# Seven sequences and one, a four-batch first run, and a half-size inverse transform in a long-convolution layer with routed experts

## The chip, the cores and the metric

The kernel runs on one core of a Trainium2 chip. Its engines are TensorE (PE in the profile; its weight loads are PEld), VectorE (DVE), ScalarE (ACT), GpSimd (POOL) and SyncE (SP, which here only starts transfers). Each engine works through its own list of instructions in order, and they meet through semaphores. The metric is the device time of one execution in microseconds. The kernel before has a median of 708.53 us over six executions, from 697.98 to 713.18.

## The reference, cut to what matters

Eight sequences of 512 tokens and 256 channels go through a gated long convolution and then a mixture of 16 experts of which each token uses 4, each with a residual and a layer norm:

```python
def layer(x):                                    # 8 x 512 x 256, float32
    u = short_conv(x @ W_in + b_in)              # 768 channels, three taps
    x0, x1, v = split(u, 3)
    k = sin-MLP filter, 512 x 256                # the same for every sequence
    y = (irfft(rfft(v * x1) * conj(rfft(k)), 1024)[:512] + filter_bias) * x0
    x = layernorm(x + y @ W_out + b_out)
    w, e = top_4(softmax(x @ gate.T))            # weights made to sum to 1
    out = sum_k w_k * (silu(x @ w1[e_k].T) * (x @ w3[e_k].T)) @ w2[e_k].T
    out += (silu(x @ sw1.T) * (x @ sw3.T)) @ sw2.T    # the shared expert
    return layernorm(x + out)
```

## The kernel before, in words

**The first half, per sequence.** `front` (from L436) projects the transposed input to 768 channels in blocks of 128 (`u_ps`, L413), applies the three taps on ScalarE and VectorE (L396 to L402), multiplies to get v, turns it (`vt_ps`, L456) and takes a forward transform as matmuls with a table of cosines and sines (`v_ps`, L479). `product` (L498 to L529) multiplies by the filter's spectrum on VectorE; its result `pf` has two halves, c = 0 and c = 1, that belong to the two halves of the 512 positions. `convolved_full` (L537) is the inverse transform: for each of two blocks of 128 channels and each half c, four float32 matmuls with a moving operand of 256 columns from the table `inv4_sb` (L547). `gated_y`, `normed` and `scaled` multiply by x0, project with W_out (`z_ps`, L630) and normalise to x1.

**Routing.** `turned` and `heads` turn x1 and compute the gate and the shared expert (`x1t_ps` L663, `hs_ps` L678, `os_ps` L782). `router` takes the top four, `route` counts how many rows each expert has got (`r_ps`, L821), and `scatter` sends each token's row to four places in HBM with 16 indirect transfers of GpSimd (L960), into a region `xs` per set in which every expert has its own stretch of rows.

**Sets and batches.** `SPLIT` (L27) groups sequences into sets, and the sequences of a set into batches. A set has its own `xs` and its own table of results in HBM. When a batch but the last of a set is routed, only tiles of 128 rows that are already full are computed; the last batch takes what remains, with partly filled tiles. `slots()` counts them: 17, 32 and 62 tiles for the batches of the first set (sequences 0 to 5), and 47 for the second set (6 and 7), 158 in all.

**The experts.** `fetch` (L1096) loads four tiles at a time (`xr`), waiting for one of two buffers. `expert_pair` handles two tiles, a pair: four transposes (`xr_ps`, L1150), eight matmul passes with w1 and w3 (`h_ps`, L1164), silu on ScalarE into `act` (L1175), a product on VectorE (L1178), two transposes of `act` back into `h_ps` (L1184), a copy to `actt` (L1189), four passes with w2 (`o_ps`, L1196), a scaling with the routing weight into `o` (L1207 or L1209), and per tile one indirect transfer to the results (L1218). `act` and `actt` have three buffers each.

**The return.** When all pairs of a set have written their results, `returned` loads for each of its sequences four blocks `got` of 512 KB (L1258), adds the four contributions of each token to the shared expert's sum, normalises and stores (`out_x`, L1307). The sum of a sequence in the first set is meanwhile kept in HBM (`kept`, L798; read back at L1242); the last set's stays on the chip. In the last set odd blocks are added by TensorE (`s_ps`, L1269).

**What sets the order.** The order on every engine is worked out when the program is built: each step names its engine, an estimated cost, what it needs and which buffers it takes, and a planner (`Plan.run`) repeatedly picks the step that can start first, and among near equals the one of lowest rank. A sequence b has rank 2 + b/100; the pairs of a batch have the rank in `late`, so that the first batch's pairs stand behind the front of sequence 3 and ahead of that of sequence 4, the second's ahead of sequence 6, the last two behind sequence 7. Nine buffers of 4 KB per partition, `b4`, serve many uses (inputs, v, y, sums, `got` and others).

Of the kernel before, what the change touches and what calls it, by code (L numbers as in the profile page):

```python
# [13 lines left out]
F32 = mybir.dt.float32  # L14
# [6 lines left out]
P = 128  # L21
# [5 lines left out]
SPLIT = (((0, 1), (2, 3), (4, 5)), ((6, 7),))  # L27
OUTRANK = 0.5
KD = D // P
# [173 lines left out]
def layer(  # L203
# [20 lines left out]
    fwd: bass.AP,  # L224
    inv4: bass.AP,
# [35 lines left out]
    plan.ring(h=4, xr=2, sel=6, xrt=3, act=3, actt=3, ob=4, at=4)  # L261
# [54 lines left out]
    load(inv4_sb, inv4.rearrange("(k p) t -> p k t", p=P), "inv4")  # L316
    b_out_sb = const.tile([P, D], F32, name="b_out_sb")
# [180 lines left out]
    def product(b, vf, hf_):  # L498
# [15 lines left out]
        plan.done(("pf", b, 0))  # L514
        plan.spawn(convolved_full(b, pf, hp), 2 + b * 0.01)
# [12 lines left out]
        plan.let(hf_)  # L528
        plan.done(("pf", b, 1))  # L529

# [6 lines left out]
    def convolved_full(b, pf, hp):  # L537
        for i in range(KD):
            for c in range(2):
                rings = [*(["ps"] if c == 0 else []), *(["b4:y"] if i == c == 0 else [])]  # L540
                yield turn("PE", 8 * PASS[CH], [("pf", b, c), "inv4"], rings)
                if i == c == 0:
                    y, hy = sb("b4:y", 0, [P, KD, T], f"y_{b}")
                if c == 0:
                    y_ps, h = ps([P, T], f"y_ps_{b}_{i}")
                for k in range(4):
                    nc.tensor.matmul(  # L547
                        y_ps[:, c * CH : (c + 1) * CH],
                        lhsT=pf[:, k // 2, k % 2, c, i * P : (i + 1) * P],
                        rhs=inv4_sb[:, k, :],  # L550
                        start=k == 0,
                        stop=k == 3,
                    )
# [519 lines left out]
    late = [2 + b * 0.01 - 0.005 for b in (4, 6, 8, 9)]  # L1073
# [51 lines left out]
    def expert_pair(p, f, xr4, hxr):  # L1125
# [48 lines left out]
        act, hact = sb("act", 3, [P, 2, HE], f"act_{p}", home=home)  # L1174
# [12 lines left out]
        actt, hat = sb("actt", 3, [P, 2, P], f"actt_{p}", home=home)  # L1187
# [141 lines left out]
def shape_constants():  # L1329
# [28 lines left out]
    found = {"places": places, "tri": tri, "seg": np.concatenate(seg), "pos": pos, "decay": decay, "fwd": fwd, "inv4": inv4, "sign": np.stack([even, -even], 1)}  # L1358
# [40 lines left out]
```

## Time and profile before

| | |
|---|---|
| median of six executions | 708.53 us (697.98 to 713.18) |
| the profiled execution | 709.05 us, with a span of 707.3 us |
| mean granted TensorE clock | 0.921 |
| PE busy | 587.0 us (83% of the span) |
| DVE / ACT / POOL busy | 458.2 / 366.8 / 319.9 us |
| moved by DMA | 114.08 MB, 161 GB/s over the span |
| last routing matmul (`r_ps`, sequence 7) | at 476.7 us |
| first load of `got` | at 589.88 us |
| last expert matmul | ends at 673.85 us |

The profile is one execution on the chip. Times are microseconds from the start of the span unless marked ns. A busy PE is not a PE at its peak: its matmuls are pipelined, and the granted clock can halve, so the distance from the start of one group of matmuls to the start of the next is a better price than the mean duration of one. A float32 matmul runs as two passes, and the profile counts passes; a transpose is one pass. The 1.75 us between the span and the execution's own time lie around the span.

### The profile page before, as it was taken

Reading aid. Unit: us, or ns where it says so; the run is one execution under the profiler, and the core shown is the slowest. Engines: PE = TensorE matmul, PEld = TensorE weight load, DVE = VectorE, ACT = ScalarE, POOL = GpSimd, SP = SyncE. Lnnn points to the kernel's source line nnn. Section 1 sums busy time; section 2 is a strip of 40 time slices with the busy share of each in tenths; the row PEclk is TensorE's granted clock in tenths of the full one; section 3 lists DMA queues with packets and bytes.
Section 4 is the critical chain, followed back from the end, with each engine's and each line's share of the span. In section 5 each row is a group of like instructions: output and inputs, shape, how many; then the busy total and the mean of one; then the engine's idle time right before and its main releaser. Section 6 shows DMA issues by size and latency. Waiting matters only on the chain.

```text
span 707.3 us, 10010 instructions
## 1 busy us (share of the span) xinstructions
PE 587.0 (83%) x2508; PEld 448.1 (63%) x2508; DVE 458.2 (65%) x1271; ACT 366.8 (52%) x810; POOL 319.9 (45%) x588
## 2 busy tenths in 40 slices
PE   6979798987969699979598996796787999899724
PEld 2437484845748577767466785685676877787612
DVE  4998989998759459958472586346132234777754
ACT  3416465654455276754242760472242445898855
POOL 0000007373563474376676238347556655456540
PEclk9999999996989799989799999798899999899968
DMA  8991003234341153335563424225524456979855
GB/s 274 355 341 36 30 31 143 81 114 148 116 152 56 62 177 125 105 149 195 174 210 119 152 88 161 75 85 203 186 96 144 139 147 207 302 264 310 310 186 205
DMA packets 67686, 114.08 MB, mean 161 GB/s; under 512 B 11547, under 2 KB 48425, under 8 KB 67630
## 3 DMA queue, kind: packets, MB, share of 16 engines
q1 hardware_dynamic: 53902, 77.75, 34.6%
q0 software_dynamic: 13728, 35.69, 13.4%
q8 instruction: 22, 0.36, 0.2%
q14 instruction: 34, 0.28, 0.1%
HBM read 61.25 MB, written 56.07 MB: 166 GB/s over the span
## 4 chain that ended last, share of the span: by engine, by line
PE 56%; DVE 15%; another core or an unknown queue 7%; ACT 7%; issue 6%; DMA 5%; POOL 3%; SPq 1%; ACTq 0%; POOLq 0%; DVEq 0%
PE h_ps L1164 13%; PE o_ps L1196 9%; PE y_ps L547 7%; PE u_ps L413 6%; PE hs_ps L678 4%; PE z_ps L630 4%; DMA got<-results 4%; PE xr_ps L1150 3%; PE v_ps L479 3%; PE h_ps L1184 2%; POOL results L1218 1%; POOL xs L960 1%; ACT unused L589 1%; PE os_ps L782 1%
## 5 line engine op out<-in xcount | busy, mean ns | idle before, releaser
L1218 POOL DMA_INDIRECT results<-o,to x158 | 161.6, 1023 | 161.5 <-ACT o L1207 63.4
L960 POOL DMA_INDIRECT xs<-x,at x128 | 135.3, 1057 | 198.6 <-DVE cx L402 106.3
L1164 PE MATMUL h_ps<-w_sb,xrt 128*128 x632 | 154.6, 391 | 12.4 <-ACT xrt L1155 10.6
L1164 PEld LDWEIGHTS h_ps<-w_sb,xrt 128*128 128x128 f32 x632 | 120.4, 197 | 31.5 <-ACT xrt L1155 12.5
L1196 PE MATMUL o_ps<-w_sb,actt 128*128 x316 | 91.0, 424 | 41.3 <-ACT actt L1189 29.5
L1196 PEld LDWEIGHTS o_ps<-w_sb,actt 128*128 128x128 f32 x316 | 63.1, 210 | 56.2 <-ACT actt L1189 34.5
L413 PE MATMUL u_ps<-xt,w_in_sb 128*128 128x512 f32 x192 | 88.8, 604 | 4.1 <-DMA xt<-in_x_t 4.1
L1178 DVE TENSOR_TENSOR act<-act,h_ps 128x256 f32<-128x256 f32 (+1 forms) x80 | 31.9, 414 | 92.7 <-ACT act L1175 67.7
L1175 ACT ACTIVATE act<-h_ps 128x256 f32<-128x256 f32 (+1 forms) x80 | 29.9, 382 | 96.8 <-remote 40.7
L547 PE MATMUL y_ps<-inv_sb,pf 128*128 128x256 f32 x256 | 65.2, 411 | 11.7 <-DVE pf L526 9.7
L396 ACT ACTIVATE u<-u_ps,chan_sb 128x512 f32<-128x512 f32 x48 | 33.1, 689 | 72.6 <-DVE v L402 32.5
L547 PEld LDWEIGHTS y_ps<-inv_sb,pf 128*128 128x128 f32 x256 | 52.4, 208 | 23.8 <-DVE pf L526 11.0
L1155 ACT COPY xrt<-xr_ps 128x512 f32<-128x512 f32 (+1 forms) x80 | 45.3, 586 | 41.4 <-PE xr_ps L1150 14.7
L413 PEld LDWEIGHTS u_ps<-xt,w_in_sb 128*128 128x128 f32 x192 | 35.9, 193 | 42.7 <-issue 41.2
L1150 PE MATMUL xr_ps<-ident,xr 128*128 128x128 f32 x316 | 47.4, 283 | 1.7 <-ACT xrt L1155 0.7
L1207 ACT ACTIVATE o<-o_ps,sel 128x256 f32<-128x256 f32 x84 | 35.0, 470 | 26.5 <-PE o_ps L1196 18.8
L1209 DVE TENSOR_TENSOR o<-o_ps,sel 128x512 f32<-128x512 f32 x37 | 25.5, 690 | 34.4 <-PE o_ps L1196 17.9
L678 PE MATMUL hs_ps<-w_sb,x1t 128*128 128x272 f32 x128 | 37.2, 449 | 10.1 <-ACT x1t L431 5.8
L1150 PEld LDWEIGHTS xr_ps<-ident,xr 128*128 128x128 f32 x316 | 39.4, 147 | 9.6 <-issue 4.1
L1189 ACT COPY actt<-h_ps 128x256 f32<-128x256 f32 (+1 forms) x80 | 28.3, 378 | 29.8 <-remote 15.0
L1184 PE MATMUL h_ps<-ident,act 128*128 128x128 f32 x158 | 30.6, 292 | 12.5 <-issue 8.2
L678 PEld LDWEIGHTS hs_ps<-w_sb,x1t 128*128 128x128 f32 x128 | 27.5, 219 | 18.0 <-ACT x1t L431 6.5
(179 smaller groups left out, 943.9 us busy)
## 6 DMA issues: line engine op xcount, KB each, us to landing
xr<-xs SPq DMA_DIRECT2D x158, 144.0 KB
got<-results SPq DMA_DIRECT2D x32, 512.0 KB
xs<-blank SPq DMA_DIRECT2D x62, 144.0 KB
w_sb<-in_experts SPq DMA_DIRECT2D x17, 384.0 KB
xt<-in_x_t SPq DMA_DIRECT2D x8, 512.0 KB
xn<-in_x SPq DMA_DIRECT2D x8, 512.0 KB
kept<-acc SPq DMA_DIRECT2D x6, 512.0 KB
sum<-kept SPq DMA_DIRECT2D x6, 512.0 KB
```

The lines of the kernel that those rows point to most:

```text
L396: nc.scalar.activation(u, u_ps, AF.Identity, bias=chan_sb[:, m, 3:4])
L413: nc.tensor.matmul(u_ps, lhsT=w_in_sb[:, k, m * P : (m + 1) * P], rhs=xt[:, k, :], start=k == 0, stop=k == KD - 1)
L547: nc.tensor.matmul(y_ps[:, c * CH : (c + 1) * CH], lhsT=pf[:, k // 2, k % 2, c, i * P : (i + 1) * P], rhs=inv4_sb[:, k, :], start=k == 0, ...
L678: nc.tensor.matmul(h_ps, lhsT=x1t[:, k, q * P : (q + 1) * P], rhs=w_sb[:, k, NE * D :], start=k == 0, stop=k == KD - 1,)
L960: move = nc.gpsimd.indirect_dma_start(out=xs[i], out_offset=bass.IndirectOffsetOnAxis(ap=at[:, q, k : k + 1], axis=0), in_=x1[:, q, :], in ...
L1150: nc.tensor.transpose(t_ps[:, j, k, :], xr[:, j, k * P : (k + 1) * P], ident)
L1155: nc.scalar.copy(xrt[:, :n], t_ps[:, :n])
L1164: nc.tensor.matmul(h_ps[:, j, :], lhsT=xrt[:, j, k, :], rhs=w_sb[:, k, bass.ds(at[j], D)], start=k == 0, stop=k == KD - 1,)
L1184: nc.tensor.transpose(a_ps[:, j, :], act[:, j, :], ident)
L1196: nc.tensor.matmul(o_ps[:, j, :], lhsT=actt[:, j, :], rhs=w_sb[:, 2, bass.ds(at[j], D)], start=True, stop=True)
L1207: nc.scalar.activation(o[:, j], o_ps[:, j], AF.Copy, scale=sel[:, j0 + j, 0:1])
L1218: move = nc.gpsimd.indirect_dma_start(out=results[i], out_offset=bass.IndirectOffsetOnAxis(ap=to[:, j0 + j : j0 + j + 1], axis=0), in_=o[: ...
```

## The change

Three edits. The sets become seven sequences and one, with the first set in four batches; from sequence 3 on (`FULL = 3`) the inverse transform uses the sum and the difference of the two halves of `pf`, with half as many columns per matmul; and `act` and `actt` have two buffers instead of three, which is the room that the second table takes. The tiles per batch are now 17, 32, 32 and 46 for the first set and 31 for the second, again 158. `late` gets one more rank: the third batch's pairs stand ahead of the front of sequence 7.

```diff
-SPLIT = (((0, 1), (2, 3), (4, 5)), ((6, 7),))
+SPLIT = (((0, 1), (2, 3), (4, 5), (6,)), ((7,),))
+FULL = 3
...
-    plan.ring(h=4, xr=2, sel=6, xrt=3, act=3, actt=3, ob=4, at=4)
+    plan.ring(h=4, xr=2, sel=6, xrt=3, act=2, actt=2, ob=4, at=4)
...
     load(inv4_sb, inv4.rearrange("(k p) t -> p k t", p=P), "inv4")
+    inv_sb = const.tile([P, 2, CH], F32, name="inv_sb")
+    load(inv_sb, inv.rearrange("(k p) t -> p k t", p=P), "inv")
...
-        plan.done(("pf", b, 0))
-        plan.spawn(convolved_full(b, pf, hp), 2 + b * 0.01)
+        if b < FULL:
+            plan.done(("pf", b, 0))
+            plan.spawn(convolved_full(b, pf, hp), 2 + b * 0.01)
...
+        if b < FULL:
+            plan.done(("pf", b, 1))
+            return
+
+        yield turn("DVE", 2 * 1.22, (), ["b4:pe"])
+        pe, he = sb("b4:pe", 0, [P, 2, 2, D], f"pe_{b}")
+        nc.vector.tensor_tensor(pe, pf[:, :, 0], pf[:, :, 1], ALU.add)
+        plan.done(("pf", b, 0))
+        nc.vector.tensor_tensor(pf[:, :, 0], pf[:, :, 0], pf[:, :, 1], ALU.subtract)
         plan.done(("pf", b, 1))
+        plan.spawn(convolved(b, (pe, pf[:, :, 0]), (he, hp)), 2 + b * 0.01)
...
+    def convolved(b, sums, held):
+        for i in range(KD):
+            for k in range(2):
+                rings = [*(["ps"] if k == 0 else []), *(["b4:y"] if i == k == 0 else [])]
+                yield turn("PE", 8 * PASS[P], [("pf", b, k), "inv"], rings)
+                if i == k == 0:
+                    y, hy = sb("b4:y", 0, [P, KD, T], f"y_{b}")
+                if k == 0:
+                    y_ps, h = ps([P, T], f"y_ps_{b}_{i}")
+                for c in range(2):
+                    for part in range(2):
+                        nc.tensor.matmul(
+                            y_ps[:, c * CH + k : (c + 1) * CH : 2],
+                            lhsT=sums[k][:, part, c, i * P : (i + 1) * P],
+                            rhs=inv_sb[:, part, k * P : (k + 1) * P],
+                            start=part == 0,
+                            stop=part == 1,
+                        )
+            plan.done(("y_ps", b, i))
+            plan.spawn(gated_y(b, i, y, y_ps, h), 2 + b * 0.01)
+        plan.let(*held)
+        plan.spawn(normed(b, y, hy), 2 + b * 0.01)
...
-    late = [2 + b * 0.01 - 0.005 for b in (4, 6, 8, 9)]
+    late = [2 + b * 0.01 - 0.005 for b in (4, 6, 7, 8, 9)]
...
-        act, hact = sb("act", 3, [P, 2, HE], f"act_{p}", home=home)
+        act, hact = sb("act", 2, [P, 2, HE], f"act_{p}", home=home)
...
-        actt, hat = sb("actt", 3, [P, 2, P], f"actt_{p}", home=home)
+        actt, hat = sb("actt", 2, [P, 2, P], f"actt_{p}", home=home)
```

The order that comes out of the planner differs between the two programs from sequence 3 on. In the order of TensorE, the pairs whose `h_ps` matmuls stand ahead of the routing matmuls of sequence 7 are 35 before and 41 after. In the order of SP, the first set's last fetch is followed by four fetches of the second set, and then the loads of `got` begin, in both programs. Before, 8 fetches and 24 loads of `got` for the first set follow, 16 of these loads ahead of the last fetch and 8 behind it; then 8 loads for the second set. After, 4 fetches and 28 loads follow, 11 ahead of the last fetch and 17 behind it; then 4 loads for the second set.

More of the change, by code (lines that the diff above doesn't have):

```diff
@@ L224, in layer @@
     fwd: bass.AP,
+    inv: bass.AP,
     inv4: bass.AP,
@@ L1357, in shape_constants @@
     places = np.concatenate([TOPK * (QT * p + np.arange(QT)) - spare, spare], 1)
[L1358 removed]
+    found = {"places": places, "tri": tri, "seg": np.concatenate(seg), "pos": pos, "decay": decay, "fwd": fwd, "inv": fwd.T / CH, "inv4": inv4, "sign": np.stack([even, -even], 1)}
     return {k: np.ascontiguousarray(v, f32) for k, v in found.items()}
```

## The prediction

> **What bounds the kernel now.** I read the page's busy times and slices first, then the busy time by stage, then single stretches of the timeline.
>
> ```profile
> PE 587.0 (83%) x2508; PEld 448.1 (63%) x2508; DVE 458.2 (65%) x1271; ACT 366.8 (52%) x810; POOL 319.9 (45%) x588
> ...
> PE   6979798987969699979598996796787999899724
> ...
> DMA  8991003234341153335563424225524456979855
> ```
>
> TensorE is the busiest, but no single engine holds for the whole span, so I cut it where the work changes: end of the front-only stretch, routing of sequence 7 (476.4), first load of results (589.9), last fetch (650.7), last expert matmul (673.9).
>
> ```profile
> core 0: us, PE busy (x) PEld busy (x) DVE busy (x) ACT busy (x) POOL busy (x), PEclk, DMA share, GB/s
> 0.00:175.00 175.00, 151.10 (x488) 94.77 (x489) 153.49 (x351) 87.76 (x168) 38.91 (x76) 0.93 0.47 156
> 175.00:476.40 301.40, 259.55 (x1171) 207.02 (x1170) 189.90 (x558) 150.81 (x340) 160.76 (x291) 0.92 0.38 129
> 476.40:589.90 113.50, 92.61 (x450) 77.66 (x449) 37.86 (x112) 41.06 (x98) 69.04 (x131) 0.92 0.47 149
> 589.90:650.70 60.80, 55.00 (x277) 46.21 (x276) 45.04 (x141) 49.88 (x109) 31.80 (x57) 0.94 0.87 291
> 673.90:707.30 33.40, 9.87 (x32) 7.19 (x32) 16.01 (x62) 16.90 (x48) 5.78 (x9) 0.76 0.53 190
> ```
>
> See three regimes. Until 175 VectorE and TensorE are both near full (153.5 and 151.1 of 175). From 175 to 590 TensorE leads (259.6 of 301.4, then 92.6 of 113.5). From 590 on DMA moves 291 GB/s at a share of 0.87 beside the experts, and from 673.9 the rest is the return of results alone. The chain of waits agrees: in its last part its two longest pieces are loads of `got`, 3.69 us at 681.81 and 9.56 us at 687.16.
>
> **The halved inverse transform.** Prices come from distances of starts at full clock:
>
> ```profile
> 273.87 5.34 PE L547 MATMUL y_ps<-inv_sb,pf 128*128 128x256 f32 x24
> 279.05 3.83 PE L678 MATMUL hs_ps<-w_sb,x1t 128*128 128x272 f32 x16
> ...
> 286.45 0.60 PE L1150 MATMUL xr_ps<-ident,xr 128*128 128x128 f32 x4
> 286.89 1.88 PE L413 MATMUL u_ps<-xt,w_in_sb 128*128 128x512 f32 x4
> ```
>
> 24 passes of 256 columns take 279.05 - 273.87 = 5.18 us, 0.216 each; 4 passes of 128 columns take 0.44, 0.11 each. A sequence has 32 passes before and after, so 6.9 us becomes 3.5. For the sequences 3 to 7 that is 5 x 3.45 = 17.2 us less on TensorE, all of it ahead of the routing of sequence 7. No trace row shows a float32 product of 128 columns written to every second column: below, the 0.098 of the routing passes of 64 columns (4 in 0.39 us at 104.57) would give 18.9; above, an unchanged 0.216 gives 0. I take 0.11, the nearest row in width, with fresh weights in each pass as here.
>
> A rule speaks against it. The Trainium skill, "TensorE: Matmul & The Clock Gate", section "Back-to-back issue gap", says that in a stream of weight loads and matmuls the spacing does not shrink in proportion to the columns: 81 ns per matmul at 128 where the isolated formula has 56 (109 at 256). By that shape this edit would save about 28 parts in 109, an estimate of 9 us instead of 17.2, and the forecast would rise by 8. The rows above, 0.11 against 0.216 with a load in each pass, do not show such a floor.
>
> VectorE gets two additions of 128x1024 per sequence, 1.22 us each by the filter products at L507 (eight, mean 1224 ns): 2.44 us. For sequence 3 they fall into the stretch where VectorE is full: +2.4 on the path. For the other four VectorE is busy 190 of 301 us and they hide; with that cover gone they cost 4 x 2.44 = 9.8. The matmuls also wait for the whole product instead of its first half, 9 operations of 0.69 us plus 1.22, 7.4 us later; expert pairs stand between in TensorE's order, so I take 0; without pairs it is at most 7.4 for each of five, 37.
>
> The second table adds 256 KB at the start. At 301 GB/s (the first 25 us) that is 0.9 us on every load behind it; the only wait for a load in the list of waits of the first 64 us ends at 8.05, for a load that SP issues earlier, so 0, at most 0.9.
>
> **Two buffers for act.** Read a steady pair of pairs:
>
> ```profile
> 560.72 1.89 PE L1164 MATMUL h_ps<-w_sb,xrt 128*128 x8
> 562.45 0.38 PE L1184 MATMUL h_ps<-ident,act 128*128 128x128 f32 x2
> 562.66 1.04 PE L1150 MATMUL xr_ps<-ident,xr 128*128 128x128 f32 x8
> 563.54 1.03 PE L1196 MATMUL o_ps<-w_sb,actt 128*128 x4
> 564.40 0.38 PE L1184 MATMUL h_ps<-ident,act 128*128 128x128 f32 x2
> ```
>
> A pair is 1.73 (`h_ps`) + 0.21 (back transposes) + 0.44 (half of the 0.88) + 0.86 (`o_ps`) = 3.24 us of TensorE. A buffer is held from silu (0.38) over the product (0.41) to the back transposes; two buffers allow two periods, 6.5 us, and that covers it: 0. If the cover is gone a silu that waits also holds what stands behind it on ScalarE, copies of `xrt` and `actt` and evictions, for which TensorE waits; up to 0.38 on each of 80 pairs is 30 us. Below nothing there is no reason for a gain.
>
> **Sets of seven and one.** Tiles stay 158 and pairs 80, so the experts cost the same. What moves is the border: the first set's pairs grow from 56 to 64 and the second's shrink from 24 to 16. Loads of results begin when the first set is through, 8 pairs later in TensorE's order: 8 x 3.24 = 25.9. So the first load moves from 589.9 to 589.9 + 25.9 - 17.2 + 2.4 = 601.0.
>
> From there SP's order decides. In it the loads stand among fetches, which wait for TensorE (waits of SP for `xr_ps` make 107.2 us in total):
>
> ```profile
> 589.88 0.83 SPq L1258 DMA_DIRECT2D got<-results  x2
> ...
> 648.69 1.37 SPq L1096 DMA_DIRECT2D xr<-xs  x3
> ...
> 663.56 6.03 SPq L1258 DMA_DIRECT2D got<-results  x4
> 673.41 4.49 SPq L1307 DMA_DIRECT2D out_x<-sum  x2
> 681.81 2.33 SPq L1258 DMA_DIRECT2D got<-results  x5
> ```
>
> Before, eight fetches take 58.8 us (589.9 to 648.7), 7.35 each; after there are four: 29.4, to 630.4, with 11 loads done. Behind the last fetch, before, 8 loads of the first set go out from 650.7 to 669.6, 2.4 us each, with one reload of a sum among them; after, 17 loads: 40.8, and a reload more than in proportion, 512 KB at 297 GB/s, 1.8: 673.0. The second set's pairs are done by then: 13.5 pairs remain at the first load (21.5 before, in 83 us, 3.86 each), so 601 + 52 = 653 and their writes some 8 us later (673.85 to 681.8 before). So the wait for them at 681.81 goes, and the return of the first set is what is late next. Then 4 loads instead of 8: from 681.81 to 696.73 eight took 14.9, 1.9 each, so 7.5, and 3.7 from issue to use (681.81 to 685.52): 684.2. From the last block's use to the end it is 10.6 (696.75 to 707.3), as before. Span 694.8; with 1.75 around it, **697 us**, against 709.05 of this execution, 1.7% less. The execution stands 0.5 us above the median, so I leave it.
>
> **Rivals.**
> - *The first set's return becomes the tail and is slow.* Before, six sequences took from 589.9 to 681.8, 15.3 us each. My sum has (673.0 - 601.0) / 7 = 10.3. At 15.3 the span ends at 601.0 + 107.1 + 7.5 + 3.7 + 10.6 = 729.9: **732**. It decides from 12.0 us per sequence on, where the end equals 709; over 14.1 it is slower by 2%. For it: ScalarE is busy 49.9 of 60.8 us in that stretch, and stores wait in SP's order ahead of loads. Against it: behind the last fetch 8 loads took 18.9, and half of ScalarE's work there is the experts', which end early.
> - *TensorE's time is not the bound, or the change does not halve it.* If strided writes keep 0.216, or stalls eat the gain, 17.2 returns: **714**.
> - *Stalls shrink.* Between 175 and 476 the chain has three pieces put down to an unknown queue, 9.99 us at 192.56, 7.78 at 232.08 and 13.70 at 432.18, beside runs of indirect transfers on GpSimd. A new order may meet two of them with TensorE full, some 17 us: **680**. It may as well make two more: 714, the case above. The runs of `scatter` are still eight.
>
> **How the numbers follow.** Forecast 0.46, stalls shrink 0.22, gain lost 0.17, slow return 0.15. The forecast's own spread is about 8 us either way. From 678 to 720 leaves out the slow return and the edges of the others, about 0.2; the unhidden bounds (9.8, 30, 37) lie in the cases above 709. The six times before spread over 15 us, so 2%, 694.4 to 722.7, is about what can be told from no change. Faster by more: most of 680 and some two fifths of the forecast, 0.39. Slower by more: most of 732 and a little of 714, 0.13. Within: 0.48.
>
> **What will show it.** `y_ps` passes of the later sequences at 0.11 us; last `r_ps` near 481 (6 more pairs ahead of it, 19.4, less 17.2, plus 2.4); first load of `got` near 601; last expert matmul near 653, then some 40 us with TensorE idle; no wait for `results` ahead of the last four loads. It is wrong if the first load comes much after 605, if loads behind the last fetch take over 3 us each, or if `act` waits for back transposes appear on ScalarE.

## The result and the profile after

The changed kernel takes 717.64 us in the median of 36 executions (703.84 to 726.03); 78 executions of the kernel before have a median of 707.46 us (697.44 to 715.47). The ratio is 1.0101, with a 95% interval of 1.0070 to 1.0132. It goes by the executions within 1.5% of each kernel's fastest; the medians of all, and the spans of the two profiled executions, lie some 10 us apart. The forecast was 697, a ratio of 0.984: the change was to win 11.5 us and, by the ratio, loses some 7.

The page of the changed kernel: busy time of each engine, then the slices of TensorE and of DMA, then the shares of the chain that ended last.

```profile
PE 570.9 (80%) x2492; PEld 435.6 (61%) x2492; DVE 470.5 (66%) x1302; ACT 365.4 (51%) x815; POOL 320.4 (45%) x588
...
PE   5979798994969598299788998688677998977503
...
DMA  8991004234252244414332535563553543599785
...
PE 50%; DVE 17%; another core or an unknown queue 10%; ACT 9%; issue 7%; DMA 3%; POOL 2%; SPq 1%; ACTq 0%; DVEq 0%; POOLq 0%
```

TensorE has lost 16.1 us of work (587.0 to 570.9) and VectorE has gained 12.3, as the edits say. But the span has grown from 707.3 to 717.7, so TensorE's idle time grew by 26 us. TensorE's row of slices, which before has no digit below 5 until the last two, now has a 4 in the tenth and a 2 in the seventeenth (287 to 305 us), and the share of the chain put down to an unknown queue went from 7% to 10%.

Busy time of each engine by stage, cut at the same events as in the prediction (routing of sequence 7, first load of `got`, and 684, behind which TensorE has almost nothing left):

```profile
core 0: us, PE busy (x) PEld busy (x) DVE busy (x) ACT busy (x) POOL busy (x), PEclk, DMA share, GB/s
0.00:175.00 175.00, 145.38 (x473) 89.86 (x474) 153.95 (x343) 84.89 (x164) 38.83 (x76) 0.94 0.49 157
175.00:499.60 324.60, 270.26 (x1293) 217.31 (x1293) 206.55 (x601) 165.54 (x375) 176.47 (x319) 0.91 0.41 134
499.60:621.70 122.10, 104.35 (x505) 88.21 (x505) 40.09 (x127) 46.23 (x114) 73.08 (x139) 0.90 0.46 144
621.70:684.00 62.30, 45.50 (x209) 35.98 (x207) 46.23 (x148) 49.30 (x111) 29.71 (x53) 0.90 0.85 286
684.00:717.70 33.70, 5.45 (x16) 4.20 (x16) 23.64 (x86) 19.46 (x54) 2.27 (x3) 0.60 0.75 269
```

The stage from 175 to the last routing is where the loss sits: 324.6 us where the forecast had 306 (to 481), with 54.3 us in which TensorE is idle, against 41.8 before. From there on the stages are near the forecast: 122.1 to the first load (forecast 120), 96.0 from the first load to the end (forecast 93.8).

The halved transform did what it says. The timeline of TensorE shows eight passes in each line:

```profile
176.28 1.05 PE L585 MATMUL y_ps<-inv_sb,pe 128*128 128x128 f32 x8
177.17 1.06 PE L585 MATMUL y_ps<-inv_sb,pf 128*128 128x128 f32 x8
178.06 1.06 PE L585 MATMUL y_ps<-inv_sb,pe 128*128 128x128 f32 x8
```

0.89 us from start to start for eight passes, 0.11 each. And this is the largest of the new stalls, from the timeline of all engines (start, length, engine and line, and in brackets the idle time ahead and what released it):

```profile
290.90 0.60 PE L1188 MATMUL xr_ps<-ident,xr 128*128 128x128 f32 x4
...
292.79 0.44 PE L1222 MATMUL h_ps<-ident,act 128*128 128x128 f32 x2 [1.29 <-issue]
...
301.47 0.96 POOL L998 DMA_INDIRECT xs<-x,at  x1 [0.22 <-issue]
...
304.64 0.59 ACT L1193 COPY xrt<-xr_ps 128x512 f32<-128x512 f32 x1 [14.29 <-remote]
...
305.28 2.07 PE L585 MATMUL y_ps<-inv_sb,pe 128*128 128x128 f32 x8 [12.05 <-ACT xrt L1193]
```

The four transposes end at 291.5. ScalarE's copy of them starts at 304.64, 2.2 us after the end of a run of 15 indirect transfers of GpSimd (283.1 to 302.4); "remote" means that the profile sees no instruction that ended just then. TensorE, next in line, waits 12.05 us for the copy. The trace of before has such waits too (the prediction's third rival names three). Waits of ScalarE and VectorE of more than 1 us with this label make 85 us before and 98 us after.

### The profile page after: what moved, and what is told of

The parts are those of the page before. It is cut to its first block, busy times and chain, and to the rows that moved or that the text cites. A ratio compares the mean times of both kernels' runs of the same rounds, so it can differ in the third digit from the quotient of the medians.

```text
span 717.7 us, 10077 instructions
## 1 busy us (share of the span) xinstructions
PE 570.9 (80%) x2492; PEld 435.6 (61%) x2492; DVE 470.5 (66%) x1302; ACT 365.4 (51%) x815; POOL 320.4 (45%) x588
## 4 chain that ended last, share of the span: by engine, by line
PE 50%; DVE 17%; another core or an unknown queue 10%; ACT 9%; issue 7%; DMA 3%; POOL 2%; SPq 1%; ACTq 0%; DVEq 0%; POOLq 0%
PE h_ps L1202 12%; PE o_ps L1234 9%; PE u_ps L417 6%; PE z_ps L668 4%; PE hs_ps L716 3%; PE xr_ps L1188 3%; PE y_ps L562 3%; PE y_ps L585 2%; PE h_ps L1222 2%; POOL xs L998 2%; ACT unused L627 2%; PE os_ps L820 1%; PE v_ps L483 1%; DVE got L1315 1%
## 5 line engine op out<-in xcount | busy, mean ns | idle before, releaser
L1202 PE MATMUL h_ps<-w_sb,xrt 128*128 x632 | 156.7, 396 | 8.9 <-issue 6.1
L1202 PEld LDWEIGHTS h_ps<-w_sb,xrt 128*128 128x128 f32 x632 | 122.9, 200 | 29.0 <-issue 7.3
L1234 PE MATMUL o_ps<-w_sb,actt 128*128 x316 | 93.5, 434 | 41.9 <-ACT actt L1227 39.0
L417 PE MATMUL u_ps<-xt,w_in_sb 128*128 128x512 f32 x192 | 91.4, 617 | 4.9 <-DMA xt<-in_x_t 4.9
L1245 ACT ACTIVATE o<-o_ps,sel 128x256 f32<-128x256 f32 x99 | 41.1, 474 | 28.1 <-PE o_ps L1234 15.7
L716 PE MATMUL hs_ps<-w_sb,x1t 128*128 128x272 f32 x128 | 34.1, 420 | 12.0 <-DVE acc L844 10.0
L1247 DVE TENSOR_TENSOR o<-o_ps,sel 128x512 f32<-128x512 f32 (+1 forms) x30 | 20.3, 681 | 33.6 <-PE o_ps L1234 16.2
L716 PEld LDWEIGHTS hs_ps<-w_sb,x1t 128*128 128x128 f32 x128 | 25.7, 204 | 19.5 <-DVE acc L844 10.4
L1227 ACT COPY actt<-h_ps 128x256 f32<-128x256 f32 (+1 forms) x80 | 28.4, 376 | 16.8 <-remote 10.7
L668 PE MATMUL z_ps<-w_out_sb,y 128*128 128x256 f32 x128 | 33.3, 411 | 4.5 <-DVE y L600 4.5
L562 PE MATMUL y_ps<-inv_sb,pf 128*128 128x256 f32 x96 | 27.1, 445 | 11.1 <-DVE pf L531 9.7
```

Source lines behind the costliest of these rows:

```text
L417: nc.tensor.matmul(u_ps, lhsT=w_in_sb[:, k, m * P : (m + 1) * P], rhs=xt[:, k, :], start=k == 0, stop=k == KD - 1)
L562: nc.tensor.matmul(y_ps[:, c * CH : (c + 1) * CH], lhsT=pf[:, k // 2, k % 2, c, i * P : (i + 1) * P], rhs=inv4_sb[:, k, :], start=k == 0, ...
L668: nc.tensor.matmul(z_ps[:, j, :], lhsT=y[:, i, q::QT], rhs=w_out_sb[:, i, :], start=i == 0, stop=i == KD - 1,)
L716: nc.tensor.matmul(h_ps, lhsT=x1t[:, k, q * P : (q + 1) * P], rhs=w_sb[:, k, NE * D :], start=k == 0, stop=k == KD - 1,)
L1202: nc.tensor.matmul(h_ps[:, j, :], lhsT=xrt[:, j, k, :], rhs=w_sb[:, k, bass.ds(at[j], D)], start=k == 0, stop=k == KD - 1,)
L1234: nc.tensor.matmul(o_ps[:, j, :], lhsT=actt[:, j, :], rhs=w_sb[:, 2, bass.ds(at[j], D)], start=True, stop=True)
```

## The experiments

The time of the kernel before depends on the chip: 697 to 710 us on most, 621 and 624 us on two. Each experiment is therefore compared with the kernel before on its own chip, by the ratio. `act_order`, `inv_all` and `pause_probe` ran on the chip with 621 us, `inv_xrt` and the three runs named `_again` on the one with 624; the others ran on chips with the longer times.

### The parts alone

`split_only` is the kernel before with the new sets and ranks, and nothing else; `inv_act` is the changed kernel with the sets and ranks of before.

```diff
 # split_only                                        # on the kernel before
+SPLIT = (((0, 1), (2, 3), (4, 5), (6,)), ((7,),))
...
+    late = [2 + b * 0.01 - 0.005 for b in (4, 6, 7, 8, 9)]
 # inv_act                                           # on the changed kernel
+SPLIT = (((0, 1), (2, 3), (4, 5)), ((6, 7),))
...
+    late = [2 + b * 0.01 - 0.005 for b in (4, 6, 8, 9)]
```

> Only the sets and the ranks change; the transform stays whole and act keeps three buffers. By the terms of the prediction the first load of results moves by the 8 pairs alone, from 589.9 to 615.8, and the end follows it by 93.8 + 1.75: 711 us. If the 19 us that TensorE lost ahead of the routing of sequence 7 come from the new order of the pairs, it is some 730. If they come from the halved transform with its additions and buffers, it stays at 711.

> Only the halved transform and the two buffers for act and actt; the sets stay six and two. By the prediction's terms TensorE gains 17.2 and VectorE costs 2.4: 694 us. If the lost 19 us belong to this part, it is 710 or more. If TensorE's time is not what sets the end ahead of sequence 7, it is 706 to 711, with the stretch up to the routing of sequence 7 as long as before (476).

Measured: the sets alone 716.72 us, ratio 1.0228 (1.0155 to 1.0301), +16 us beside 701.13. Transform and buffers 700.95 us, 0.9961 (0.9910 to 1.0013), so -3 us or nothing. The prediction's terms give +3 for the sets (-11.5 in all, less -14.8) and -14.8 for transform and buffers. Both are off by some 12 us, in the same direction.

### Two buffers: a wait or an order?

`act_only` takes the two buffers away from the kernel before. `act_order` tells the planner that there are two, so that the order of every engine is that of `act_only`, but leaves three in place. `inv_xrt` has the halved transform and three `act` and `actt` buffers, and takes the room from `xrt`.

```diff
 # act_only, on the kernel before
+    plan.ring(h=4, xr=2, sel=6, xrt=3, act=2, actt=2, ob=4, at=4)
...
+        act, hact = sb("act", 2, [P, 2, HE], f"act_{p}", home=home)
+        actt, hat = sb("actt", 2, [P, 2, P], f"actt_{p}", home=home)
 # act_order, on the kernel before
+    plan.ring(h=4, xr=2, sel=6, xrt=3, act=2, actt=2, ob=4, at=4)
-        assert n == bufs and ...
+        assert n <= bufs and ...
 # inv_xrt, on inv_act
+    plan.ring(h=4, xr=2, sel=6, xrt=2, act=3, actt=3, ob=4, at=4)
... (and the three buffer counts where the tiles are made)
```

> The kernel before with two buffers instead of three for act and actt, nothing else. The kernel with the halved transform and two buffers (and the sets of before) stood at -0.2 us where the terms of the prediction gave -14.8 (-17.2 on TensorE, +2.4 for the additions). Theory A, the buffers eat the gain: this kernel is 10 to 15 us slower than before (711 to 716 beside 701), with longer waits of ScalarE's act and actt for a free buffer. Theory B, the prediction's zero for the buffers holds: within 3 us of before (698 to 704), and the gain of the halved transform went elsewhere.

> The kernel before, with the order of instructions that the planner makes for two act and actt buffers (the order of the run with two buffers, instruction by instruction), while three buffers of each are there, so that no instruction waits for the taking back of a buffer that before did not wait. The run with two buffers was 1.0168 of before. If the cost is in waits for a buffer (the cover that the prediction counted on is gone): this kernel is within 3 us of before (0.996 to 1.004). If it is in the order that the planner makes when it believes in two buffers: within 4 us of the run with two buffers (1.011 to 1.022). Between: shared.

> The halved transform from the fourth sequence on, three act and actt buffers as before, and the place for the second table taken from xrt (two buffers instead of three), sets of before: 35 pairs stand ahead of the last routing instead of 36. If the loss beside the transform is peculiar to act and actt: 0.975 to 0.985 of before (-14.6 in full). If any buffer less makes the planner give an order that costs some 12 us: 0.993 to 1.005. If xrt, which stands first in an expert's chain, matters more: above 1.005.

Measured: `act_only` 1.0168 (1.0086 to 1.0250), `act_order` 1.0176 (1.0121 to 1.0230), `inv_xrt` 1.0306 (1.0237 to 1.0375). With three buffers really there and only the planner's belief changed, the cost is 1.8%: an order alone can cost as much as the two buffers do. The prediction argued about the waiting for a buffer. `act_order` has hardly more of it than the kernel before on a chip of the same kind: ScalarE's silu waits for back transposes three times, 7.7 us together, beside three times and 6.5 us in `before_again`. But `act_only` ran on a chip with late signals (710 us) and `act_order` on one without (621 us), so how much of the cost of `act_only` is order and how much waiting is not shown on one chip. In the order for two buffers the transposes of 37 pairs instead of 36 stand ahead of the last routing on TensorE, one pair more stands ahead of the first load of results too (242 transposes of `xr` for 238), and everything behind is arranged anew. Taking the room from `xrt` instead is dearer: 1.0306 against 1.0031 for two `act` and `actt` buffers on the same chip (`inv_act_again`, below). Whether that is order or waits for `xrt` was not separated.

### What the saving on TensorE is worth

`half_work` prices the saving by itself: order, buffers and waits of before, but the inverse transform of sequences 3 to 7 (counted from 0; its expectation counts from 1) adds two of its four terms and leaves the others out.

```diff
+                terms = range(4) if b < 3 else (0, 3)
-                for k in range(4):
+                for k in terms:
```

> The kernel before, in its own order and with all its buffers, in which the inverse transform of sequences 4 to 8 adds two of its four terms and leaves the other two out: 80 passes of 0.216 us less on TensorE, 17.3 us, no addition on VectorE, no other wait, and the planner reckons as before. It prices what the prediction took for the halved transform by itself. If TensorE sets the time up to the first load of got, as the prediction had it: 0.974 to 0.980 of before (-14 to -18), on a chip without late signals nearer to the whole. If what TensorE saves stands idle because its neighbours in a sequence's chain are not earlier: 0.990 to 1.000.

Measured: 691.99 us beside 696.92, ratio 0.9955 (0.9923 to 0.9986): -3.1 us, between -1.0 and -5.4. TensorE has 17.3 us less to do, no other instruction is changed, and the time falls by a fifth of that. This is the term that the prediction counted in full. The busy times of its page, beside 587.0 us of TensorE in the kernel before:

```profile
PE 569.2 (82%) x2428; PEld 430.6 (62%) x2428; DVE 457.0 (66%) x1271; ACT 366.6 (53%) x810; POOL 323.2 (47%) x588
```

The kernel before has no profile from that chip, so where the other 14 us went is not seen there. The granted clock of its executions is 0.924 in the mean, beside 0.933 for the kernel before: up to some 5 us (an estimate, 1% of the 569 us of work) may have gone into slower matmuls and not into idle time. The values differ with two terms left out, and so which rows go to which expert, but the bytes moved do not (114.06 MB beside 114.08).

Four more kernels keep three buffers and still halve the transform. `inv_all` halves it for all eight sequences, so that the table of the whole one is not needed; the others take every second column of the whole table (from the fifth, the third and, with the new sets, the sixth sequence on).

```diff
 # inv_all, on inv_act with three buffers
+FULL = 0
...
-    inv4_sb = const.tile([P, 4, CH], F32, name="inv4_sb")
 # inv_strided_f4, _f2 (FULL = 4, 2), after_strided_f5 (FULL = 5, new sets), with three buffers
...
-                            rhs=inv_sb[:, part, k * P : (k + 1) * P],
+                            rhs=inv4_sb[:, 2 * part, k::2],
```

> The sets of before, three act and actt buffers, and the halved transform for all eight sequences, so that the table of the whole one (512 KB, 4 KB of each partition) goes and the buffers fit. By the runs so far the halved transform from the fourth sequence on is worth -14.6 (the run with it and two buffers at -2.7 less the run with two buffers at +11.9). Three more sequences halve 32 passes each: 3 x 32 x 0.106 = 10.2 us less TensorE, against 3 x 2.4 = 7.2 us of additions on VectorE, which leads in those stages. If buffers and transform add up as measured: 0.972 to 0.985 of before. If the first three sequences stand on VectorE alone: they give the additions back, 0.985 to 0.995. If the buffers were not what took the gain in the run with both: 0.995 to 1.005.

> Sets of before and three act and actt buffers. The halved transform from the fifth sequence on (four sequences) takes its table as every second column of the whole one, cos and sin of the lower half, so that no second table is loaded and no buffer has to go; 34 pairs stand ahead of the last routing instead of 36. TensorE's work falls by 4 x 3.8 = 15.1 us (the transform's 18.9 for five sequences beside before_again). If the loss was the order for two buffers alone: 0.975 to 0.985 of before. If the passes over every second column take longer than 0.11 us: above that by 0.001 for each 0.005 us of a pass. If the gain goes into TensorE's idle time as it did with two buffers (16 of 15): 0.997 to 1.005.

> The same from the third sequence on (six sequences): TensorE's work falls by 22.7 us, two of the six stand in the stages that VectorE leads and give back 2.5 us each. If the loss was the order for two buffers alone: 0.966 to 0.980 of before. If every change of the planner's inputs costs some ten us by its order: 0.985 to 1.0.

> The sets of the change and three act and actt buffers, the halved transform from the sixth sequence on (three sequences), its table every second column of the whole one; 41 pairs ahead of the last routing as in the changed kernel. TensorE's work falls by 11.3 us. If sets and transform add up as the prediction had it (+3 and the saving less what stands idle): 0.985 to 0.995 of before on a chip without late signals. If the order takes the gain: 0.998 to 1.010. With late signals some 0.010 to 0.015 more for the sets.

Measured: `inv_all` 1.0260 (1.0205 to 1.0315), `inv_strided_f2` 1.0268 (1.0172 to 1.0364, with executions from 705.17 to 729.55), `after_strided_f5` 1.0184 (1.0066 to 1.0302). `inv_strided_f4` has a median of 704.40 beside 697.33 and executions from 689.37 to 709.06, which decides nothing but excludes no small gain. The passes over every second column take 0.115 us (eight of them 0.92), so they aren't the reason. No arrangement of the halved transform beat the kernel before by more than the noise. That the missing buffers alone had eaten the gain, as the ratios of `inv_act` and `act_only` suggested, is not borne out: with three buffers the gain does not come either. Each of these kernels has an order of its own, though, and what that order costs is in its ratio.

### Late signals of TensorE

The wait of 14.29 us above led to a theory: TensorE's signals reach the other engines late beside a long run of indirect transfers. (The profile models the ends of matmuls, so it does not tell a late signal from a matmul that itself ends late; "late signal" stands for both here.) `after_pause` breaks the runs of `scatter` into groups of four by 27 short memsets on GpSimd. `signal_probe` has, beside such runs, a thin chain of one transpose and one copy at a time; in `dense_probe` TensorE has further products to do in each step and is fed without a gap as long as the copies come in time.

```diff
 # after_pause, in scatter, on the changed kernel
+                if k == 0 and q:
+                    for _ in range(27):
+                        nc.gpsimd.memset(between, 0.0)
 # a step of dense_probe
+            nc.tensor.transpose(t_ps[:, :P], src, ident)
+            nc.scalar.copy(mid, t_ps[:, :P])
...
+            for j in range(2):
+                nc.tensor.matmul(f_ps[:, :D], lhsT=ident, rhs=w[:, at_w], start=j == 0, stop=j == 1)
+            src = mid
```

> The changed kernel; in scatter GpSimd rests for 27 memsets of one element, some 2.4 us, behind every four indirect transfers of a sequence, 7.2 us per sequence in all. Theory of late signals: signals of TensorE reach the other engines only when a long run of indirect transfers ends; with runs of four the stalls put down to an unknown queue fall from 10% of the chain to under 5%, no wait on TensorE's signal lasts over 7 us, and the time falls from 717.6 to 705 or less. Rival, the new order itself holds TensorE (buffers, VectorE) and the unknown queue is only a label: 717 or more, since GpSimd is later by 58 us in all.

> Leaves the whole computation out and stores zeros. Nine phases, each a chain of 30 steps of a transpose on TensorE and a copy on ScalarE (or copies on VectorE and ScalarE), beside: nothing; a run of 16 indirect transfers; the same with the VectorE chain; groups of four with 27 and with 13 short memsets between; memsets only; a run of 16 with 12 loads of 512 KB; loads alone; the run and loads with the VectorE chain. Late signals: the TensorE chain stands still for most of the run of 16 (over 8 us), for under 6 us with groups of four, and the chain of VectorE goes on. Rival (no such effect of GpSimd, the stalls need the kernel's own order): no step of any chain is over 2 us. If it needs traffic, only the phases with loads show it.

> Leaves the whole computation out and stores zeros. Eight phases of 22 steps: TensorE transposes (ScalarE copies the result, the next transposition waits for the copy) and multiplies two blocks of 256 columns in each step, so that it is never empty. Phase 1 alone; 2 beside a run of 16 indirect transfers; 3 the same with target rows 12 apart; 4 with the weights' place from a register; 5 with VectorE busy; 6 with ten loads of 512 KB; 7 the run cut into groups of four by memsets; 8 loads and no indirect transfers. If TensorE's signals come late beside a long run of indirect transfers (theory S), ScalarE's wait for the transposition is over 4 us once or more in phase 2 and in those behind it, and not in 1, 7 and 8; the phase in which it begins tells what it needs beside the run. If the late signals come from something else in the layer: no wait over 4 us in any phase, as in the probe before.

`after_pause` took 740.74 us, 1.0540 (1.0463 to 1.0616). As a cure it failed, and neither the time nor the longest wait came as the theory had them: its 24 pauses of about 4 us each hold GpSimd up, its waits with the label "remote" of more than 1 us still make 95 us (98 in the changed kernel), and the longest is 13.6 us. But all of them of over 2.5 us lie beside, or just behind, unbroken runs of eight transfers and more, which the writes of results still make; beside the runs of four there is none. That speaks for the theory, but pauses that move the waits without lessening them do not show what the waits cost.

In `signal_probe`, on the chip on which `split_only` has 83 us of such waits, no signal of TensorE was late: the chain keeps its 0.83 us per step beside a run of 16. In `dense_probe` it is, in all five phases with a run of 16, and already in the plainest (phase 2: contiguous target rows, no loads, no other engine). ScalarE's copies of that phase, beside a run from 28.4 to 48.5:

```profile
36.41 0.27 ACT L91 COPY mid<-t 128x128 f32<-128x128 f32 x1 [0.71 <-PE f L95]
38.44 0.27 ACT L91 COPY mid<-t 128x128 f32<-128x128 f32 x1 [1.76 <-PE f L95]
41.25 0.27 ACT L91 COPY mid<-t 128x128 f32<-128x128 f32 x1 [2.55 <-PE f L95]
46.91 0.27 ACT L91 COPY mid<-t 128x128 f32<-128x128 f32 x1 [5.39 <-remote]
51.18 0.27 ACT L91 COPY mid<-t 128x128 f32<-128x128 f32 x1 [4.00 <-remote]
52.01 0.27 ACT L91 COPY mid<-t 128x128 f32<-128x128 f32 x1 [0.57 <-PE t L89]
```

A step takes 0.97 us for the first 8 us of the run, then 2.0, 2.8, 5.7 and 4.3, and from 2.7 us behind the run on the signals are in time again. With the run cut into groups of four by pauses, the same chain has no wait longer than 2.3 us, and that one is not for TensorE.

`pause_probe` was to find what the delay grows with (passes of 128, 256 and 512 columns) and how short a pause would do.

```diff
+PHASES = ((16, 16, 0, 256, 2), (16, 16, 0, 128, 4), (16, 16, 0, 512, 1), (16, 1, 4, 256, 2), ...)
```

> Leaves the whole computation out and stores zeros. Eight phases of 40 steps of the probe before (transposition, ScalarE's copy, products on TensorE), each beside 16 indirect transfers: 1 in one run, products of 256 columns; 2 the same with 128 columns, so twice the passes in the same time; 3 with 512 columns, half the passes; 4 a pause of 4 short memsets (0.5 us) behind each transfer; 5 of 8 (1 us) behind each; 6 of 8 behind two; 7 of 13 (1.6 us) behind four; 8 of 27 (3.4 us) behind eight. If the late signals come from something that fills with TensorE's instructions while the run lasts: ScalarE's first wait over 3 us comes about 12 us into the run in phase 1, in half that time in phase 2 and late or not at all in phase 3; and the pauses help as far as they empty it. If it fills with the transfers themselves: it begins at the same transfer (the ninth to eleventh) in phases 1 to 3, and phases 4 to 6 are free of it where the pause lets a transfer finish.

It ran on the chip with 621 us, and there no signal was late in any phase. The page's busy times are these:

```profile
PE 315.8 (98%) x1680; PEld 256.9 (80%) x1680; DVE 2.7 (1%) x11; ACT 86.4 (27%) x321; POOL 161.4 (50%) x564
```

ScalarE's copies in the timeline, beside the run of 16 of the first phase (3 to 23 us):

```profile
14.20 0.27 ACT L73 COPY mid<-t 128x128 f32<-128x128 f32 x1 [0.71 <-PE t L71]
15.17 0.27 ACT L73 COPY mid<-t 128x128 f32<-128x128 f32 x1 [0.71 <-PE t L71]
```

TensorE is never held up, and a step takes 0.97 us right through the run. Its questions stay open. That `dense_probe` shows late signals and this one none, at the same chain, says that they belong to some chips and not to all.

### The same comparison where signals are not late

> The kernel before, once more with a profile, so that the three kernels beside it can be compared with a profile of the same chip. Where waits for TensorE's late signals are there: 700 to 712, with 60 to 90 us of such waits of ScalarE and VectorE; where they are not: 617 to 628, the last routing 30 to 45 us earlier than 476, the first load of got at about 505.

> The changed kernel, once more. By the runs so far the parts add up to: transform -14.6, order for two buffers +11.9, sets +15.6 (or +9.8, by the changed kernel less the run with transform and two buffers), together +7 to +13. On a chip with late signals: 1.007 to 1.018 of before. On one without them: if the parts' costs are in order and count of work, the same, 1.010 to 1.025; if the sets cost what they do through late signals, below 1.005.

> The halved transform from the fourth sequence on with two act and actt buffers and the sets of before, once more. It stood at 0.9961 of before. If transform (-14.6) and order (+11.9) are what they were: 0.991 to 1.003 again. If the halved transform pays only where late signals hold TensorE up: 1.010 to 1.020 on a chip without them, as for the order alone (1.0176).

They came to the other chip without late signals; not one wait in these profiles is longer than 0.8 us with the label "remote". The kernel before takes 623.89 us there. Measured: the changed kernel 625.82, ratio 1.0032 (0.9997 to 1.0066); transform and buffers with the sets of before 624.73, 1.0031 (0.9996 to 1.0067). So the sets cost nothing there, and transform and buffers together are worth nothing there either. Stages of the kernel before, cut at its own last routing and first load:

```profile
0.00:175.00 175.00, 148.91 (x483) 93.45 (x484) 153.62 (x351) 86.94 (x167) 39.44 (x76) 0.93 0.46 155
175.00:423.10 248.10, 244.48 (x1175) 198.70 (x1175) 188.76 (x559) 152.66 (x342) 162.67 (x291) 1.00 0.46 157
423.10:509.70 86.60, 83.39 (x451) 72.34 (x450) 37.76 (x112) 41.01 (x99) 69.20 (x131) 1.00 0.61 196
509.70:624.50 114.80, 85.11 (x403) 70.65 (x401) 76.73 (x251) 87.44 (x205) 50.33 (x91) 0.86 0.78 269
```

Here TensorE is the bound without a doubt: 327.9 of 334.7 us between 175 and the first load, 6.8 idle. On the chip of the first profile the same stretch took 414.9 (589.9 - 175): 352.2 busy, at a granted clock of 0.92 instead of 1.00, and 62.7 idle. The changed kernel:

```profile
0.00:175.00 175.00, 146.38 (x474) 90.39 (x475) 153.74 (x343) 86.00 (x165) 40.61 (x76) 0.93 0.47 158
175.00:436.90 261.90, 253.19 (x1293) 207.65 (x1292) 205.58 (x601) 164.09 (x374) 177.75 (x316) 0.99 0.48 161
436.90:532.50 95.60, 91.87 (x501) 80.06 (x500) 39.75 (x126) 45.85 (x113) 74.31 (x142) 1.00 0.62 197
532.50:624.10 91.60, 51.64 (x229) 41.71 (x227) 70.31 (x234) 69.05 (x166) 32.28 (x56) 0.79 0.84 294
```

and with the transform and two buffers alone, up to its first load:

```profile
0.00:175.00 175.00, 145.38 (x484) 89.56 (x485) 154.15 (x346) 86.23 (x166) 39.37 (x76) 0.95 0.47 158
175.00:413.10 238.10, 223.10 (x1128) 181.26 (x1127) 193.00 (x559) 148.86 (x334) 155.43 (x271) 0.99 0.45 153
413.10:510.70 97.60, 92.89 (x501) 80.56 (x500) 41.10 (x124) 47.80 (x116) 80.04 (x151) 1.00 0.61 198
```

In the last one TensorE's work ahead of the first load falls from 476.8 to 461.4 us, 15.4 less, and its idle time rises from 32.9 to 49.3, 16.4 more. The first load comes at 510.7 instead of 509.7. Of the new idle time 2.6 us are the additions ahead of sequence 3 (`hs_ps` waits for `acc` 10.8 instead of 8.2); the rest is a dozen short waits for VectorE, ScalarE and loads: 3.5 us for `actt`, 2.5 for `acts`, 2.4 for `act`, 2.1 for the routing mask, 2.0 for `xr`, 1.7 for `xrt`.

### Ranks

`after_rank` gives the third and fourth batch later ranks, so that the pairs of both stand behind the front of the last sequence.

```diff
-    late = [2 + b * 0.01 - 0.005 for b in (4, 6, 7, 8, 9)]
+    late = [2 + b * 0.01 - 0.005 for b in (4, 6, 8, 9, 9)]
```

> The changed kernel with the ranks of the third and fourth batch of experts put behind sequences 7 and 8 instead of 6 and 7: 34 pairs of experts stand ahead of the last routing on TensorE instead of 41, the work is the same. If TensorE's work ahead of the first load of got sets the time: the last routing moves up by 7 pairs x 3.24 = 22.7 us to about 477, the first load of got stays at 622 within 5, and the time is within 5 us of the changed kernel's (1.010 to 1.014 of before). If the loss of the change is in stalls that depend on which GpSimd run meets which pair: any time from 700 to 725 on a chip where before takes 704, with the busy time of TensorE unchanged (571) and its idle time different by more than 8 us.

Measured: 1.0206 (1.0119 to 1.0292). The last routing did move up, to 475.8, but the first load went back to 633.3: neither expectation holds. TensorE's busy time is 579 instead of 571 at a lower granted clock (0.895 instead of 0.901), its idle time 148 beside 147 (two profiles that need not be of one chip). An earlier last routing was worth nothing here.

## Why the prediction was wrong

**What held.** The price of a pass: 0.11 us. The rule weighed against it, of the Trainium skill's "TensorE: Matmul & The Clock Gate", "Back-to-back issue gap", has 81 ns at 128 columns in a stream of matmuls, beside 109 at 256 by its formula for a lone one, so well over half. Measured is 0.11 against 0.216 us, here as in the prediction's rows, and the passes save 16.5 us or more and not the 9 of that estimate. The additions cost some 2.6 us ahead of sequence 3 (on the chip without late signals) and the wait for the whole product costs nothing (no `y_ps` pass of the changed kernel waits for `pe`). From the routing of sequence 7 on, the account holds to some 2 us in each of its two stages. Inside the last one the experts are later than it said: the last expert matmul ends 57.7 us behind the first load, at 679.4, where the prediction had 52 and 653. The last write of results (685.1) is still ahead of the second set's loads (from 696.2), so it does not set the end. Four fetches take 28.3 us from the first load to the last fetch (29.4); this is SP's timeline there and near the end, where the first set's last loads go out:

```profile
621.68 1.32 SPq L1296 DMA_DIRECT2D got<-results  x3
...
649.92 1.39 SPq L1134 DMA_DIRECT2D xr<-xs  x3
...
691.70 4.87 SPq L1296 DMA_DIRECT2D got<-results  x5
697.58 0.34 SPq L1345 DMA_DIRECT2D out_x<-sum  x1
698.01 1.80 SPq L1296 DMA_DIRECT2D got<-results  x2
```

The rival of a slow return asked for 15.3 us a sequence; it is (695.8 - 621.7) / 7 = 10.6, near the 10.3 of the sum. Stalls did not shrink.

**The step that failed first: "17.2 us less on TensorE, all of it ahead of the routing of sequence 7", taken as time.** The work did fall: ahead of the first load `y_ps` is 16.5 us less in the profile after, 19.2 on the chip without late signals. But 17.3 us of the same passes taken out of the kernel before, at its own order, shortened it by 3.1. Of the three rivals, the one that the gain of TensorE is lost, at 714, is the one that came. That its time is so near is partly luck: by the ratios of the parts some 12 us of the miss lie in transform and buffers, and some 7 in the sets, which that rival did not touch. The sign stood in the prediction's own table: between 175 and 476 TensorE was idle for 41.8 of 301.4 us, with VectorE, the next busiest, at 63%. Idle time of the busiest engine means that something else decides part of the stretch, and there its saved work need not buy anything. The prediction counted stalls as a thing that might shrink or grow, not as a thing that swallows a saving in front of it. That a stall which ends with GpSimd's run does swallow it is the reading that fits (the stall of the changed kernel and that of `inv_act`, 4 us earlier, both end 2.1 to 2.2 us behind the same run of 15), but it was not isolated. On the chip without such stalls transform and two buffers won nothing either, with 15.4 us less work and 16.4 us more idle time ahead of the first load; there the order for two buffers, 1.8% by `act_order`, may be what took the gain. The two were not separated.

**The second: the sets at +3.** On the chip without late signals this was right (1.0032 against 1.0031). Where signals are late the sets cost 1.4% (1.0101 against 0.9961) to 2.3% (`split_only`). Part of it is a count: nine pairs more, not eight, stand ahead of the first load (274 transposes of `xr` instead of 238), at 3.57 us of busy time each where the sum had 3.24, 32.1 us for 25.9. The rest may be their place. The kernel before takes 80 us longer between 175 and the first load on the chip with late signals (414.9 against 334.7 us) and only 3 behind it (117.4 against 114.8). The sets move pairs out of the stretch that differs little into the one that takes 24% longer: an estimate of 8 us for 32.1 us of work, beside a measured difference of some 10. No run tests this by itself.

**The third: "two periods, 6.5 us, and that covers it: 0".** The bound of 0 to 30 us held, the value did not: +11 by itself (1.0168 and 1.0176). What `act_order` pays for is another thing than the one costed: an order, not a wait. The waits foreseen do appear as well (ScalarE's `act` for the back transposes: none before, four after, 8.4 us together; on the chip without late signals 6.5 us before and 18.1 after). What they cost was not measured. In combination with the transform the order is yet another, so these 11 us do not simply add: transform and buffers together are at -3 where signals are late and at +2 where they are not.

**The sums beside each other**, difference of after and before, in us, from the profiles:

| | forecast | chip of the first profiles | chip without late signals |
|---|---|---|---|
| TensorE's work ahead of the first load | +8.7 | +16.7 | +14.6 |
| TensorE idle ahead of the first load | +2.4 | +15.1 | +8.1 |
| first load to the end | -23.6 | -21.4 | -23.1 |
| span | -12.5 | +10.4 | -0.4 |

Without late signals the miss is 12 us: 5.9 in TensorE's work, most of it the ninth pair, and 5.7 in its idle time. On the chip of the first profiles some 11 more are lost, 7 of them as idle time of TensorE; its granted clock is 0.901 instead of 0.921 there, and 0.944 instead of 0.956 on the other chip.

**What stays open.** What swallows the saving is not shown: that the same work taken out buys a fifth of itself is measured on a chip with late signals, what it is worth on one without them, at the order of before, is not. Why the planner's order for two buffers is dearer was not followed further than the one pair.

## What to carry to other kernels

The busiest engine is not the bound of a stretch in which it idles for a seventh of the time: before counting a saving on it as time, take the same work out at an unchanged order and see what comes back. Where a planner makes the order, a changed buffer count or cost is a new order on every engine, here worth 1.8% with nothing else altered; test that by itself before arguing about waits. And work that moves across a border (here, the first load of results) is priced by what a microsecond of it costs on the other side.

## What the runs showed of the hardware

- Beside an unbroken run of indirect transfers of GpSimd a densely fed TensorE's signals reach ScalarE and VectorE late. In a bare loop the first long wait begins seven to eleven transfers into a run of 16, waits last up to 7.5 us, and it is over within 3 us of the run's end. A thin chain (one transpose every 0.83 us) and runs of four with pauses of 4 to 6 us show none of it. Whether the signal or the matmul itself is late the profile does not tell.
- It depends on the chip. On two chips the profiles show none, and the kernel before took 621 and 624 us there instead of 697 to 710. That the late signals are what makes the whole difference was not tested. What limits the signals, and whether the recording of profiles has a part in it, is not known from these runs.
